# The end of a convolution, attention and expert kernel: the outputs of the experts sorted on TensorE, a new order of the two layers, and more weight buffers

## The chip, the cores and the metric

The kernel runs on one core of a Trainium2 chip. The metric is the device time of one execution in microseconds; the time of a kernel is the median of several runs. Engines are named as in the profile: PE (TensorE), PEld (its weight loads), DVE (VectorE), ACT (ScalarE), POOL (GpSimd), SP (SyncE, which here issues every DMA).

## The reference, cut to what matters

Eight images of 128 channels by 36 by 36 pass through a convolution and attention layer, then through an additive attention over 1296 tokens, and last through a layer of 64 experts, each of which picks 8 tokens of an image. Only the last part is touched in substance:

```
def _L1_ffn_ref(x, gate_w, gate_b, weight1, weight2):
    logits = jnp.einsum('bsd,ed->bse', x, gate_w) + gate_b
    probs = jax.nn.softmax(logits, axis=1)
    vals, idx = jax.lax.top_k(probs.transpose(0, 2, 1), K)      # K = 8 tokens of 1296
    ...
    pooled = jnp.einsum('bked,bke->bed', gathered, topv)        # one row per image and expert
    h = jnp.concatenate([pooled.transpose(1, 0, 2), ones], axis=-1)
    h = jax.nn.gelu(jnp.einsum('ebd,edh->ebh', h, weight1), approximate=False)
    h = jnp.concatenate([h, ones], axis=-1)
    out = jnp.einsum('ebh,eho->ebo', h, weight2)
    ...
    outputs = outputs.at[jnp.arange(Bn)[:, None], flat_idx].add(weighted)   # back to the tokens, by topv
    return outputs
```

`weight1` is 64 experts of 129 x 512 floats and `weight2` is 64 of 513 x 128; the last row of each is a bias. Without the biases they are 32 MiB, and every byte is read once. The result is added to the residual and written as 8 images of 128 x 1296 floats (5.3 MB).

## The kernel before

The order of each engine's instructions is written out by hand: generators are advanced in turn, and nothing is rescheduled afterwards. All DMAs stand in one queue, SP's, in program order. A DMA that must wait for something holds up every DMA behind it. Eight semaphores serve the DMAs in rotation, so each DMA also waits until the one eight places before it has landed.

The long part is the additive attention of layer 1. It is cut into units (image, third of the queries, tile of keys), each unit into 12 slots. In a slot PE makes a denominator `d` and a numerator `n` (L963), ACT takes the logarithm and exponential (`lq`, L986 and L989), and DVE multiplies (L1006 to L1017). The products of four slots are summed on DVE in `accd`, those of the other eight by POOL in `accp` (L1024, L1026). At the end of a unit `sums` folds the two halves of `accp` together and adds `accd`, both on POOL (L1033, L1035), and ACT makes the weights `e` (L1046). The key factors `kf` are loaded two units ahead by `prefetch` (L946). Images overlap: while image b is in this loop, image b+1 goes through its convolutions in the background, which read the padded windows `xwin`.

After the last unit, pools of the loop (`score`) are closed and the pool `wts`, 9 buffers of 1 MiB, takes their place. Nine weight loads are issued (L1202 for `weight1`, L1204 for `weight2`), then the biases, the last piece of the layer's input, 24 loads of gates `gd` (L1224) and the residuals `res` (L1229, L1241). Between these stands the store of image 7's gates (L879). Meanwhile the gating of image 7 ends in `pooled` (L901).

The experts are then worked off in 16 groups of four. For a group there are three steps:

- `inner`: bias by a matmul with a selector `which`, then the first layer, then Gelu on ACT (L1255, L1258, L1261);
- `turned`: four transposes of the hidden values and a copy by DVE (L1268, L1270);
- `outer`: the second layer, 32 matmuls (L1280); four groups share a PSUM bank, and DVE copies it out once in four groups (L1284).

One pass of the loop over g does `outer(g - 2)`, `turned(g - 1)`, `inner(g)` and issues up to two weight loads. Loads stand in the queue as w1[g], w2[g-2], w1[g+1], and so on.

The outputs come out with the image along partitions (32 rows for each of four experts, 8 of them used). They are needed with the expert along partitions, for two images at a time. The kernel writes them to DRAM in one order (`eod`, L1299, four DMAs) and reads them back in another (`eo`, L1305, four DMAs), and DVE adds the second bias (L1306). Last, for each pair of images and each third of the tokens, PE multiplies by the gates (`pf`, L1314), DVE adds to the residual (L1317, 24 times), and an image is stored when its three thirds are done (L1319).

Of the kernel before, what the change touches and what calls it, by code (L numbers as in the profile page):

```python
# [10 lines left out]
F32 = mybir.dt.float32  # L11
# [9 lines left out]
CH = 432  # L21
# [51 lines left out]
def kernel(  # L73
# [53 lines left out]
    ident = const.tile([128, 128], F32, tag="ident", name="ident")  # L127
    make_identity(nc, ident)

    eod = dram.tile([NB, E, O], F32, tag="eod", name="eod")  # L130

    with ExitStack() as loop, ExitStack() as score:

        def pool(name, bufs, stack=loop, side="left", space=bass.MemoryType.SB):
# [4 lines left out]

        big = pool("big", 8, ctx)  # L140
        etp = pool("etp", NKT + 1, ctx)
        chunks = pool("chunks", 8)
        one = pool("one", 1)
        two = pool("two", 2)
        kfp = pool("kfp", 3, score, "right")
        kstp = pool("kstp", 3, score, "right")
# [755 lines left out]
            yield matmuls()  # L902

        res = []

        def residuals(n):

# [83 lines left out]
        def numerators(p):  # L991
            ns = [ps_n.tile([128, 512], F32, tag="n", name="n") for _ in range(banks(*slots[p]))]
            products(*slots[p], 1, ns)
            return [ps[:, :CH] for ps in ns]

        def terms(p, ns):

            u, k = slots[p]
            g, o = group_of[p]
            lq = lq_of[g]  # L1000
            mult = nc.vector.tensor_mul
            rem = units[u][2] == NKT - 1
            if k in DVE_PAIRS and not rem:
                if k == DVE_PAIRS[0]:
                    live["d"] = acc.tile([128, CH], F32, tag="accd", name="accd")
                    mult(live["d"], ns[0], lq[:, o, :])  # L1006
                    mult(ns[1], ns[1], lq[:, o + 1, :])
                    nc.vector.tensor_add(live["d"], ns[1], live["d"])
                else:
                    for h in range(2):  # L1010
                        mult(ns[h], ns[h], lq[:, o + h, :])  # L1011
                    for h in range(2):
                        nc.vector.tensor_add(live["d"], ns[h], live["d"])  # L1013
            else:
                rp = rpp.tile([128, 2, CH], F32, tag="rp", name="rp")
                for h, n in enumerate(ns):
                    mult(rp[:, h, :], n, lq[:, o + h, :])  # L1017
                if rem:
                    live.setdefault("rem", []).extend(rp[:, h, :] for h in range(len(ns)))
                elif k == 0:  # L1020
                    live["r"] = rp
                elif k == 2:
                    live["p"] = acc.tile([128, 2, CH], F32, tag="accp", name="accp")
                    nc.gpsimd.tensor_add(live["p"], live["r"], rp)  # L1024
                else:
                    nc.gpsimd.tensor_add(live["p"], live["p"], rp)  # L1026
            if p in ends:
                lq_of.pop(g)

        def sums(u):  # L1030

            s = live.pop("p")
            nc.gpsimd.tensor_add(s[:, 0, :], s[:, 0, :], s[:, 1, :])  # L1033
            d = live.pop("d")
            nc.gpsimd.tensor_add(d, s[:, 0, :], d)  # L1035
            return d

        es = {}
# [132 lines left out]
        while pending:  # L1171
# [10 lines left out]
        biases = ctx.enter_context(tc.tile_pool(name="biases", bufs=1, side="right"))  # L1182
# [6 lines left out]
        w1s, w2s = {}, {}  # L1189
# [28 lines left out]
        gates = [[etp.tile([128, CH], F32, tag="e", name="gates") for _ in range(NCH)]  # L1218
# [13 lines left out]


    last = ctx.enter_context(tc.tile_pool(name="last", bufs=1))

    def aux(name):
        return ps_last.tile([128, 512], F32, tag="aux", name=name)

    for b in range(len(res), NB):
        res.append(big_tile("res")[:, :N])  # L1240
        nc.sync.dma_start(res[b], t2d[b])  # L1241
    load_gates(NB - 1)

    out_s = last.tile([128, NGR, O], F32, tag="out_s", name="out_s")
    hidden, hidden_t, sums_of = {}, {}, {}

    def inner(g):
        ph = aux("phid")
# [14 lines left out]

    def turned(g):
        x = hidden.pop(g)
        pt = aux("phT")
        for c in range(NHC):
            nc.tensor.transpose(pt[:, c * 128 : (c + 1) * 128], x[:, c::NHC], ident)  # L1268
        xt = hidp.tile([128, NHC, 128], F32, tag="hidT", name="hidT")
        nc.vector.tensor_copy(xt.rearrange("p c b -> p (c b)"), pt)  # L1270
        hidden_t[g] = xt

    def outer(g):
        xt = hidden_t.pop(g)
        if g % 4 == 0:
            sums_of[0] = aux("pout")
        po = sums_of[0][:, (g % 4) * O : (g % 4 + 1) * O]
        for c in range(NHC):
            for q in range(EG):
                mm(po[32 * q : 32 * q + 32, :], xt[:, c, 32 * q : 32 * q + 32],  # L1280
                   w2s[g][:, q, c * O : (c + 1) * O],
                   start=(c == 0), stop=(c == NHC - 1))
        if g % 4 == 3:
            nc.vector.tensor_copy(  # L1284
                out_s[:, g - 3 : g + 1, :], sums_of[0].rearrange("p (g o) -> p g o", o=O)
            )

    for g in range(NGR + 2):
        if 0 <= g - 2:
            outer(g - 2)  # L1290
        if 0 <= g - 1 < NGR:
            turned(g - 1)
        if g < NGR:
            inner(g)
        for _ in range(min(1 + (g >= 2), len(to_load))):
            load_next()
    eods = eod.rearrange("b (g q) o -> q b g o", q=EG)
    for q in range(EG):
        nc.sync.dma_start(eods[q], out_s[32 * q : 32 * q + NB])  # L1299


    eos = []
    for h in range(NB // 2):
        eos.append(last.tile([128, O], F32, tag=f"eo{h}", name="eo"))
# [77 lines left out]
```

## Time and profile before

| | us |
|---|---|
| median of 3 runs | 6135.24 (6124.2 to 6139.08) |
| the profiled execution, its own time | 6138.18 |
| its span in the profile | 6136.4 |
| end of the last unit's sums on POOL (L1035) | at 5989.43 |
| first weight load issued | at 5984.71 |
| `pooled` of image 7 copied (L901) | at 6017.86 |
| first `pf` matmul | at 6115.78 |
| first output store issued | at 6120.67 |

Times "at" are counted from the start of the span. Up to about 5985 us the kernel is in the main loop, where PE is the busiest engine (92% over the whole span); from there on it is in the part described last. In the profile's tables by stage each row has a stretch of time, its length, the busy time of PE, PEld, DVE, ACT and POOL with the number of instructions, the granted PE clock (1.00 is full speed), the busy share of the 16 DMA engines, and GB/s. In the chain of waits each row has a start, a duration and what the end of the run was waiting for at that time.

### The profile page before, as it was taken

To read this page: it belongs to the slowest core of one execution; us is meant where nothing else is said; L and a number is where in the kernel's file an instruction comes from. 1 tells how busy PE (TensorE), PEld (TensorE's weight loads), DVE (VectorE), ACT (ScalarE), POOL (GpSimd) and SP (SyncE) were. 2 spreads that over 40 slices of the span, in tenths; PEclk is the share of its full clock that TensorE was granted. 3 is DMA by queue.
4 is the path that set the end of the run, shared out by engine and by line. 5 is a ranking of instruction groups with operands and counts; after the bars stand their busy time and mean duration, and the time that the engine had idled before them with its cause. 6 is when DMAs were issued, how large, how long until landed. Compare 5 with 4: busy or idle time off the path is not lost.

```text
span 6136.4 us, 94187 instructions
## 1 busy us (share of the span) xinstructions
PE 5669.6 (92%) x33480; PEld 2924.0 (48%) x33480; DVE 4787.2 (78%) x9521; ACT 5331.3 (87%) x5851; POOL 4595.9 (75%) x2819
## 2 busy tenths in 40 slices
PE   7999999999999999999999999999999999988886
PEld 5554455544554445544445444454455544534433
DVE  4787878878788788877788777887878878788882
ACT  1999898998989989889998999899998998999990
POOL 4777777787778867778687777877777777777870
PEclk9999999999999999999999999999999999999997
DMA  1200021001110011100111001110011001110008
GB/s 44 73 34 22 25 75 39 20 25 33 67 38 20 26 47 52 37 24 26 59 37 42 22 20 65 40 37 22 25 67 47 21 25 33 57 49 26 28 20 297
DMA packets 151528, 270.95 MB, mean 44 GB/s; under 512 B 45648, under 2 KB 76752, under 8 KB 151056
## 3 DMA queue, kind: packets, MB, share of 16 engines
q1 hardware_dynamic: 151056, 264.92, 13.0%
q8 instruction: 264, 4.33, 0.3%
q14 instruction: 208, 1.70, 0.1%
HBM read 200.41 MB, written 64.19 MB: 43 GB/s over the span
## 4 chain that ended last, share of the span: by engine, by line
PE 54%; DVE 16%; ACT 15%; issue 11%; POOL 2%; DMA 1%; SPq 0%; DVEq 0%; ACTq 0%; POOLq 0%
PE d L963 18%; PE n L963 12%; ACT lq L986 11%; PE pa L286 7%; DVE rp L1017 7%; DVE n L1011 5%; PE pc L286 5%; PE s L286 3%; DVE accd L1013 2%; PE pq L286 2%; PE pk L286 1%; PE d L968 1%; PE n L968 1%; ACT e L1046 1%; DMA w<-in_weight_dram 1%
## 5 line engine op out<-in xcount | busy, mean ns | idle before, releaser
L1026 POOL TENSOR_TENSOR accp<-accp,rp 128x864 f32<-128x864 f32 x1440 | 2912.8, 2023 | 989.4 <-DVE rp L1017 946.2
L963 PE MATMUL d<-qf,kf 32*128 32x432 f32 (+1 forms) x11520 | 2791.6, 563 | 264.8 <-ACT lq L986 259.6
L963 PE MATMUL n<-qf,kf 32*128 32x432 f32 (+1 forms) x11520 | 3001.7, 556 | 28.4 <-DVE rp L1017 10.0
L986 ACT ACTIVATE lq<-d 128x864 f32<-128x864 f32 x2928 | 2481.1, 877 | 471.2 <-PE n L963 288.8
L1017 DVE TENSOR_TENSOR rp<-n,lq 128x432 f32<-128x432 f32 x3912 | 2182.0, 601 | 760.7 <-PE n L963 606.0
L989 ACT ACTIVATE lq<-lq 128x864 f32<-128x864 f32 (+1 forms) x1944 | 2495.9, 1284 | 61.6
L963 PEld LDWEIGHTS d<-qf,kf 32*128 32x128 f32 (+1 forms) x11520 | 1026.4, 185 | 1445.5 <-ACT lq L986 1106.0
L963 PEld LDWEIGHTS n<-qf,kf 32*128 32x128 f32 (+1 forms) x11520 | 1263.3, 186 | 700.1 <-issue 293.8
L1013 DVE TENSOR_TENSOR accd<-n,accd 128x432 f32<-128x432 f32 x1440 | 867.8, 603 | 24.7
L1011 DVE TENSOR_TENSOR n<-n,lq 128x432 f32<-128x432 f32 x1440 | 810.8, 607 | 58.3 <-PE n L963 36.8
L1024 POOL TENSOR_TENSOR accp<-rp 128x864 f32<-128x864 f32 x240 | 485.1, 2021 | 290.3 <-DVE rp L1017 287.7
L286 PE MATMUL pa<-xh,e 128*108 128x129 f32 x1920 | 254.8, 281 | 35.2 <-DVE accd L1013 28.0
L286 PEld LDWEIGHTS pa<-xh,e 128*108 128x108 f32 x1920 | 221.0, 174 | 129.9 <-DVE accd L1013 103.0
L1035 POOL TENSOR_TENSOR accd<-accp,accd 128x432 f32<-128x432 f32 x240 | 266.1, 1109 | 18.8
L1033 POOL TENSOR_TENSOR accp<-accp 128x432 f32<-128x432 f32 x240 | 264.7, 1103 | 11.9
L713 POOL TENSOR_SCALAR qf<-qf,cs_s 128x432 f32<-128x432 f32 x192 | 260.0, 1364 | 9.3 <-ACT qf L712 9.3
L464 POOL TENSOR_TENSOR tot<-tot,e 116x432 f32<-116x432 f32 x192 | 212.2, 1105 | 9.0 <-ACT e L473 4.6
L286 PE MATMUL s<-q,k 128*116 128x432 f32 x480 | 207.0, 547 | 8.1 <-DVE accd L1013 5.6
L473 ACT ACTIVATE e<-s 116x432 f32<-116x432 f32 x240 | 116.1, 520 | 99.3 <-PE s L286 98.1
L286 PE MATMUL pa<-e,vw 116*128 116x432 f32 x480 | 196.8, 532 | 0.5
L286 PEld LDWEIGHTS pk<-xT,a_k 128*128 128x128 f32 x1408 | 164.9, 193 | 54.2 <-DVE accd L1013 43.5
L1006 DVE TENSOR_TENSOR accd<-n,lq 128x432 f32<-128x432 f32 x240 | 144.1, 600 | 50.1 <-PE n L963 29.7
(213 smaller groups left out, 3796.2 us busy)
## 6 DMA issues: line engine op xcount, KB each, us to landing
kf<-kd SPq DMA_DIRECT2D x239, 512.0 KB
kd<-ks SPq DMA_DIRECT2D x158, 256.0 KB
w<-in_weight_dram SPq DMA_DIRECT2D x32, 1024.0 KB
wk_t<-wk_t_d SPq DMA_DIRECT2D x7, 768.0 KB
wv_t<-wv_t_d SPq DMA_DIRECT2D x7, 768.0 KB
wq_t<-wq_t_d SPq DMA_DIRECT2D x7, 768.0 KB
x<-in_x_dram SPq DMA_DIRECT2D x8, 648.0 KB
t<-tokd SPq DMA_DIRECT2D x96, 54.0 KB
```

What stands on the lines that cost most here:

```text
L286: mm(out, lhsT, rhs, **kw)
L713: nc.gpsimd.tensor_scalar(qf[:, 1, :], qf[:, 0, :], cs_s[:, q : q + 1], None, ALU.mult)
L963: mm(outs[h][:, :CH], kf[rows[h], q, :], qf_of[b, c, q][rows[h], part, :], start=True, stop=True)
L986: nc.scalar.activation(lq[:, o : o + n, :], d[:, :n, :CH], AF.Ln)
L989: nc.scalar.activation(some, some, AF.Exp, scale=-1.0)
L1011: mult(ns[h], ns[h], lq[:, o + h, :])
L1013: nc.vector.tensor_add(live["d"], ns[h], live["d"])
L1017: mult(rp[:, h, :], n, lq[:, o + h, :])
L1024: nc.gpsimd.tensor_add(live["p"], live["r"], rp)
L1026: nc.gpsimd.tensor_add(live["p"], live["p"], rp)
L1033: nc.gpsimd.tensor_add(s[:, 0, :], s[:, 0, :], s[:, 1, :])
L1035: nc.gpsimd.tensor_add(d, s[:, 0, :], d)
```

## The change

Five edits, all in the last part or for its sake:

1. The first group's `weight1`, both biases and so one of the 32 weight loads move forward to the start of image 7's units. They go into `xwin`, which no later convolution needs; the pool `one` is kept open for that.
2. `wts` has 10 buffers, and 10 loads are issued at once (the first of them is now w1[1]).
3. In the very last unit the last addition into `accp` and the two additions of `sums` are done by DVE, not POOL.
4. In the loop over groups `inner(g)` stands ahead of `outer(g - 2)`. Each group's output is copied out by itself, transposed by PE, and copied by DVE to its place in `by_image`. After the loop four more transposes give the expert along partitions, and DVE adds the bias straight from PSUM. `eod` and its eight DMAs are gone. A second PSUM pool of four banks, `ps_more`, is added.
5. In the last stage 8 of the 24 additions to the residual are done by POOL, from a copy that ACT makes (`held`).

```diff
@@ the pools @@
         etp = pool("etp", NKT + 1, ctx)
+        one = pool("one", 1, ctx)
         chunks = pool("chunks", 8)
-        one = pool("one", 1)
...
+        w1s, w2s, ffn_bias = {}, {}, []
+        def first_weights():
+            t = one.tile(list(xwin.shape), F32, tag="xwin", name="w0").rearrange(
+                "p j n -> p (j n)"
+            )
+            w1s[0] = t[:, : EG * HID].rearrange("p (e h) -> p e h", e=EG)
+            nc.sync.dma_start(w1s[0], weight1[:EG, :128, :].rearrange("e d h -> d e h"))
+            b1_s = t[:E, EG * HID : (EG + 1) * HID]
+            nc.sync.dma_start(b1_s, weight1[:, 128, :])
+            b2_s = t[:, (EG + 1) * HID : (EG + 1) * HID + O]
+            for h in range(2):
+                nc.sync.dma_start(b2_s[E * h : E * (h + 1)], weight2[:, HID, :])
+            ffn_bias.extend((b1_s, b2_s))
...
+        def ending(u):
+            return nc.vector if u == len(units) - 1 else nc.gpsimd
...
-                    nc.gpsimd.tensor_add(live["p"], live["p"], rp)
+                    ending(u if k == NP - 1 else 0).tensor_add(live["p"], live["p"], rp)
...
-            nc.gpsimd.tensor_add(s[:, 0, :], s[:, 0, :], s[:, 1, :])
+            ending(u).tensor_add(s[:, 0, :], s[:, 0, :], s[:, 1, :])
             d = live.pop("d")
-            nc.gpsimd.tensor_add(d, s[:, 0, :], d)
+            ending(u).tensor_add(d, s[:, 0, :], d)
...
                     if b == NB - 1:
                         gates.append(residuals(4))
+                        first_weights()
...
-            tc.tile_pool(name="wts", bufs=9, side="right", reuse_waits="tile")
+            tc.tile_pool(name="wts", bufs=10, side="right", reuse_waits="tile")
...
-        for g in range(NGR + 2):
+        for g in range(1, NGR + 2):
...
-        for _ in range(9):
+        for _ in range(10):
             load_next()
-        b1_s = biases.tile([E, HID], F32, tag="b1", name="b1_s")
-        nc.sync.dma_start(b1_s, weight1[:, 128, :])
-        b2_s = biases.tile([128, O], F32, tag="b2", name="b2_s")
-        for h in range(2):
-            nc.sync.dma_start(b2_s[E * h : E * (h + 1)], weight2[:, HID, :])
+        b1_s, b2_s = ffn_bias
...
     def outer(g):
         xt = hidden_t.pop(g)
-        if g % 4 == 0:
-            sums_of[0] = aux("pout")
-        po = sums_of[0][:, (g % 4) * O : (g % 4 + 1) * O]
+        po = aux("pout")[:, :O]
...
-        if g % 4 == 3:
-            nc.vector.tensor_copy(
-                out_s[:, g - 3 : g + 1, :], sums_of[0].rearrange("p (g o) -> p g o", o=O)
-            )
+        of_group = ends_p.tile([128, O], F32, tag="outs", name="outs")
+        nc.vector.tensor_copy(of_group, po)
+        outs.append((g, of_group))
+
+    def sort_outs():
+        g, of_group = outs.popleft()
+        pt = aux("poT", ps_more)[:, :128]
+        nc.tensor.transpose(pt, of_group, ident)
+        nc.vector.tensor_copy(
+            by_image[:, :, g * EG : (g + 1) * EG].rearrange("o b q -> o q b"),
+            pt.rearrange("o (q x) -> o q x", q=EG)[:, :, :NB],
+        )
 
     for g in range(NGR + 2):
+        if g < NGR:
+            inner(g)
         if 0 <= g - 2:
             outer(g - 2)
         if 0 <= g - 1 < NGR:
             turned(g - 1)
-        if g < NGR:
-            inner(g)
+        if len(outs) > 1 or g == NGR + 1:
+            sort_outs()
         for _ in range(min(1 + (g >= 2), len(to_load))):
             load_next()
-    eods = eod.rearrange("b (g q) o -> q b g o", q=EG)
-    for q in range(EG):
-        nc.sync.dma_start(eods[q], out_s[32 * q : 32 * q + NB])
+    while outs:
+        sort_outs()
 
     eos = []
     for h in range(NB // 2):
+        pt = aux("peo", ps_more)[:, :O]
+        nc.tensor.transpose(
+            pt, by_image[:, 2 * h : 2 * h + 2, :].rearrange("o b e -> o (b e)"), ident
+        )
         eos.append(last.tile([128, O], F32, tag=f"eo{h}", name="eo"))
-        nc.sync.dma_start(eos[h], eod[2 * h : 2 * h + 2].rearrange("b e o -> (b e) o"))
-        nc.vector.tensor_add(eos[h], eos[h], b2_s)
+        nc.vector.tensor_add(eos[h], pt, b2_s)
...
-            pfs = [aux("pf")[:, :CH] for _ in range(2)]
+            pfs = [aux("pf", of)[:, :CH] for of in (ps_last, ps_more)]
...
                 r = res[2 * h + i][:, cols]
-                nc.vector.tensor_add(r, pfs[i], r)
+                if i == 1 and c < NCH - 1:
+                    held = ends_p.tile([128, CH], F32, tag="held", name="held")
+                    nc.scalar.activation(held, pfs[i], AF.Copy)
+                    nc.gpsimd.tensor_add(r, held, r)
+                else:
+                    nc.vector.tensor_add(r, pfs[i], r)
```

More of the change, by code (lines that the diff above doesn't have):

```diff
@@ L128 @@
     make_identity(nc, ident)
-    eod = dram.tile([NB, E, O], F32, tag="eod", name="eod")
     with ExitStack() as loop, ExitStack() as score:
@@ L1178 @@
         wts = ctx.enter_context(
-            tc.tile_pool(name="wts", bufs=9, side="right", reuse_waits="tile")
+            tc.tile_pool(name="wts", bufs=10, side="right", reuse_waits="tile")
         )
         hidp = ctx.enter_context(tc.tile_pool(name="hidp", bufs=2, side="right"))
-        biases = ctx.enter_context(tc.tile_pool(name="biases", bufs=1, side="right"))
         ps_last = ctx.enter_context(
@@ L1185 @@
         )
-        w1s, w2s = {}, {}
         to_load = deque()
-        for g in range(NGR + 2):
+        for g in range(1, NGR + 2):
             if g < NGR:
@@ L1234, with aux @@
     last = ctx.enter_context(tc.tile_pool(name="last", bufs=1))
-    def aux(name):
-        return ps_last.tile([128, 512], F32, tag="aux", name=name)
+    ends_p = ctx.enter_context(tc.tile_pool(name="ends", bufs=2))
+    ps_more = ctx.enter_context(
+        tc.tile_pool(name="ps_more", bufs=4, space=bass.MemoryType.PSUM)
+    )
+    def aux(name, of=ps_last):
+        return of.tile([128, 512], F32, tag="aux", name=name)
     for b in range(len(res), NB):
@@ L1242 @@
     load_gates(NB - 1)
-    out_s = last.tile([128, NGR, O], F32, tag="out_s", name="out_s")
-    hidden, hidden_t, sums_of = {}, {}, {}
+    by_image = last.tile([O, NB, E], F32, tag="by_image", name="by_image")
+    hidden, hidden_t, outs = {}, {}, deque()
     def inner(g):
@@ L1265, in turned @@
         x = hidden.pop(g)
-        pt = aux("phT")
+        pt = aux("phT", ps_more)
         for c in range(NHC):
@@ L1292 @@
             turned(g - 1)
-        if g < NGR:
-            inner(g)
+        if len(outs) > 1 or g == NGR + 1:
+            sort_outs()
         for _ in range(min(1 + (g >= 2), len(to_load))):
             load_next()
-    eods = eod.rearrange("b (g q) o -> q b g o", q=EG)
-    for q in range(EG):
-        nc.sync.dma_start(eods[q], out_s[32 * q : 32 * q + NB])
+    while outs:
+        sort_outs()
     eos = []
     for h in range(NB // 2):
+        pt = aux("peo", ps_more)[:, :O]
+        nc.tensor.transpose(
+            pt, by_image[:, 2 * h : 2 * h + 2, :].rearrange("o b e -> o (b e)"), ident
+        )
         eos.append(last.tile([128, O], F32, tag=f"eo{h}", name="eo"))
-        nc.sync.dma_start(eos[h], eod[2 * h : 2 * h + 2].rearrange("b e o -> (b e) o"))
-        nc.vector.tensor_add(eos[h], eos[h], b2_s)
+        nc.vector.tensor_add(eos[h], pt, b2_s)
     for h in range(NB // 2):
```

## The prediction

> **What bounds the kernel now.** I read the table by stage first, over the stretch after the main loop, since every edit lies there (the main loop's instructions keep their order on every engine but for four loads on SP).
>
> ```profile
> 6017.00:6024.00 7.00, 6.28 (x19) 2.56 (x19) 0.70 (x2) 0.60 (x1) 0.29 (x1) 0.50 0.60 164
> 6044.00:6100.00 56.00, 42.57 (x489) 21.55 (x482) 9.17 (x14) 5.97 (x10) 2.58 (x9) 0.94 1.04 384
> 6106.00:6116.00 10.00, 0.21 (x2) 0.24 (x4) 0.58 (x2) 0.00 (x0) 0.00 (x0) 0.63 0.29 47
> 6121.00:6131.00 10.00, 8.40 (x33) 4.41 (x30) 9.42 (x19) 0.00 (x0) 0.00 (x0) 1.00 0.96 378
> ```
>
> From 6044 to 6100 the DMA engines are full at 384 GB/s: the weights set the pace, PE has 13 us to spare. Before that there is a hole at 164 GB/s, from 6106 to 6116 every engine stands nearly still, and from 6121 the output stores fill the DMA engines again. The chain of waits says what the end hangs on in each piece.
>
> ```profile
> 5985.09 2.00 POOL accp L1026
> 5987.16 1.10 POOL accp L1033
> 5988.34 1.09 POOL accd L1035
> ...
> 6083.31 14.52 DMA w<-in_weight_dram
> 6097.83 0.14 issue
> 6097.96 1.08 PE pout L1280 x32
> 6099.04 0.68 PE phT L1268 x4
> 6099.72 1.05 PE phid L1255 x2
> 6100.77 0.99 PE phid L1258 x8
> 6101.77 0.87 PE pout L1280 x32
> ...
> 6104.11 1.12 PE pout L1280 x32
> 6105.26 0.70 DVE out_s L1284
> ...
> 6108.33 4.98 DMA eod<-out_s
> ```
>
> A load takes 14.5 us from issue to landing, so some five are under way and the number of buffers does not limit the steady part. PE starts `outer` on a fresh load at 6081.73, 6087.15, 6092.55 and 6097.96: 5.41 us for two loads, 2.7 each. Two loads follow the one of 6097.83, so the last lands at about 6103.2. Last, the waits of SP's own queue, for what holds the loads up:
>
> ```profile
> SPq L1202 <- POOL accp L1026: 6.8, 1, 6.8
> SPq L1224 <- DMA w<-in_weight_dram: 6.2, 3, 2.8
> SPq L1241 <- DMA gd<-gt: 4.5, 1, 4.5
> ```
>
> The first weight load waits for POOL to have read an `rp` buffer (issue at 5984.71). Then nine loads fill the DMA engines; three gates trickle out behind landing weights; the other 18, then `res`, the store of gates and its landing (4.5 us) keep SP until 6033.86, when the tenth load is issued.
>
> [...]so all of SP's queue stands behind a waiting load. The trace agrees (the 4.5 us at L1241). [...]the four 64 KB stores of `eod` need 4.98 us from the last issue. [...] The trace shows 0.63 from 6106 to 6116 and 1.00 again from 6121.
>
> **Part by part.**
>
> *Last sums on DVE.* Before: 2.00 + 1.10 + 1.09 us on POOL to 5989.43. After: DVE ends the last `rp` at 5984.94 and adds 864, 432 and 432 elements. DVE's 64x1296 SBUF addition (L878) takes 1499 ns, 1.16 ns an element, so 1.0 + 0.6 + 0.6 = 2.2 us, end at 5987.2. The weights `e`, and `pooled` behind them, come 2.2 us earlier. I cost that at nothing for the end: the store of image 7's gates is issued at 6025.03 though its data are ready at 6010.9 (SP is not there yet), and PE's group work is far enough ahead of the loads at 6034. That cover is SP's gate loads; without them it would be worth 2.2 us.
>
> *Tenth buffer.* The tenth buffer makes the pool reach further into the memory of the closed pools. In the changed kernel as built, the first load waits for the last of these DVE additions, because it now overlaps `accd`. So it goes out at 5987.2, not 5984.71: a new wait of **+2.4 us**, and every load and gate is behind it.
>
> *Loads.* Before the gates there are ten loads instead of nine (+2.7) and no biases (192 KB at 384 GB/s, -0.5): the last one before the stall lands +4.6 later. By then six gates have gone out instead of three, as each waits only for an older load; 15 instead of 18 follow, at 0.64 us each (SP's rows of the timeline: 18 issues from 6012.3 to 6024.3, one of them 0.7 longer): -2.0. SP reaches the store of gates, its 4.5 us wait and the next weight load **+2.6 us** later, at 6036.5. But 21 loads are left instead of 23: -5.4. The last load lands at 6100.4, **-2.8 us**. The early load costs 1.2 MB, 3.2 us of DMA time, at the start of image 7; `kf` is loaded two units ahead, a unit takes over 20 us and DMA is 10 to 20% busy there: nothing.
>
> *Order of the loop.* `outer(13)` to `outer(15)` were held by PE, not by the load: `inner(15)` stood between them, and the last `outer` ended at 6105.2, 2.0 us after its load. Now `inner(g)` uses the load that lands first, and `outer(15)` starts on its landing: end 0.14 + 1.08 = 1.2 after it. The added transposes and copies (16 of each, 0.3 us) lie in PE's and DVE's waits for loads; PE has 13 us of idle in 56, they need 5.
>
> *Sorting.* After that `outer`, with 0.06 for a hand-over between engines: DVE copy 0.29 (like L772, 108x129), transpose 0.34 (L1268), DVE copy 0.27 (L901), first of four transposes 0.34, bias 0.29 (L1306), the first pair of `pf` 0.99 (four 64x432 matmuls of L963 in the timeline), two more pairs at 0.9, one DVE addition 0.6. Sum 1.2 + 0.35 + 0.4 + 0.33 + 0.4 + 0.35 + 0.99 + 1.8 + 0.6 = 6.4 us from the landing to the first store. Before: 6120.67 - 6103.2 = 17.5. **-11.1 us**, of which the DRAM trip is some 9.
>
> *Shared additions.* DVE needed 24 x 0.52 us; POOL takes 8 of them at 1.1 us (L1033) after an ACT copy. I count nothing for it beyond the first store: from the first store's issue to the end are 15.7 us, and 5.3 MB at 378 GB/s are 14.0 of them. The stores are the bound, and remain it. POOL ends its eighth addition at 4.0 + 0.65 + 8.9 = 13.6 us after the landing, while the last store's turn comes at about 19; the second store, which waits for POOL's second, is ready 0.6 us after the first, inside the first's 1.7.
>
> **Sum.** -2.8 - 11.1 = -13.9 us. Against the profiled execution's own 6138.18: 6124.3. That one lies 2.9 over the median 6135.24, so the median becomes 6121.3. That is 0.23%; 0.3%, about what a measurement of this kernel can tell from no change, would be 18.4 us.
>
> **Rivals.**
> - *The loads gain in full.* If the first load does not wait for the sums in effect, or the gates hide behind the tenth load, the stream gains up to 5.9 us, and with a quicker hand-over in the sorting the sum is -17 to -20: 6115 to 6118. For it: SP's 0.64 us gates leave the DMA engines at 164 GB/s. Against it: SP stands in order.
> - *Half clock at the end.* The sorting leaves PE little to do for 2 us; if the clock falls, the pairs of `pf` take 1.8 us, above the 1.1 that the stores need, for 3 to 10 us (both lengths occur): +3 to +6, 6124 to 6128. For it: the clock fell to half at 6043 and 6071 in the loop.
> - *Slower.* The early load stands in SP's queue ahead of `kf`. If its buffer were still being read, all of image 7's `kf` loads would wait; slower by 0.3% needs a stall of 32 us, so a hold of over 70. Against it: the last read of `xwin` is at 5019, over 200 us earlier.
> - *No change at all.* All of it hidden: excluded by the 10 idle us before 6116 on the chain.
>
> **Chances.** The sum as worked out 0.55 (its own range 6116 to 6127), full gain 0.25, half clock 0.15, slower 0.03, the rest unexplained. The bound lies at 6116.8, in the full gain and the lower edge of the sum, to which the runs' own spread of 15 us adds: faster 0.29, within 0.68, slower 0.03. The range reaches from 6109 to 6131.
>
> **What would show it.** Right: first load issued near 5987, next load after the gates near 6036.5, last `pout` ending near 6101.6, first `pf` near 6103.4, first store near 6106.8, span near 6122.5, no `eod`. Wrong: a first load at 5984.7, an end that hangs on POOL `res` or on PE `pf` at half clock, or main loop times that moved.

## The result, and the profile after

The changed kernel takes 6122.38 us in the median of 22 runs, against 6132.9 us of the kernel before, also 22 runs: a ratio of 0.9983, interval 0.9977 to 0.9989, that is 10.5 us less (7 to 14). The profiled execution took 6131.19 us with a span of 6129.5.

Executions of one and the same kernel differ by some 20 us. Nearly all of it arises in the main loop, which the change leaves alone: in the profiled executions shown here its last `rp` addition on DVE ended between 5972.8 and 5990.4 us, later where the record of the granted clock has more time at half clock (116 us of it in the one case, 172 in the other). In the profile before it ended at 5984.94, in the profile after at 5989.94. All places below are therefore counted from the end of that addition, and **the rest** is the time from there to the end of the span: 151.5 us before, 139.5 after.

| us after the last `rp` | before | predicted | after |
|---|---|---|---|
| first weight load issued | -0.2 | 2.3 | 2.5 |
| last load of the first row landed (9th, after: 10th) | 27.3 | 31.9 | 35.0 |
| next weight load, behind the gates | 48.9 | 51.6 | 54.3 |
| last weight load landed | 118.2 | 115.5 | 117.7 |
| first `pf` matmul | 130.8 | 118.5 | 120.7 |
| first output store issued | 135.7 | 121.9 | 123.8 |
| end (the rest) | 151.5 | 137.6 | 139.5 |

The table by stage of the changed kernel, with the columns as before (stretch, length, busy PE, PEld, DVE, ACT, POOL, PE clock, DMA share, GB/s):

```profile
6025.00:6035.00 10.00, 10.00 (x70) 3.56 (x73) 1.68 (x3) 2.83 (x4) 0.86 (x3) 0.77 0.58 155
...
6050.00:6106.00 56.00, 42.22 (x497) 22.01 (x497) 11.29 (x31) 5.38 (x9) 2.02 (x7) 0.91 1.03 380
6107.00:6113.00 6.00, 4.71 (x52) 2.91 (x54) 2.77 (x9) 1.06 (x2) 0.70 (x1) 1.00 0.01 3
6114.00:6124.00 10.00, 5.58 (x32) 2.70 (x28) 6.66 (x13) 3.10 (x6) 6.93 (x7) 0.89 0.95 375
```

The hole at the gates is still there, 155 GB/s for 10 us. The ten idle microseconds before the last stage are gone: from 6107 to 6113 the DMA engines rest, but PE is busy 4.71 of 6 us, at full clock. The chain of waits shows what it does, from the landing of the last load to the first `pf`:

```profile
6092.79 14.86 DMA w<-in_weight_dram
6107.65 0.14 issue
6107.78 1.11 PE pout L1294 x32
6108.90 0.02 issue
6108.92 0.30 DVE outs L1298
6109.23 0.04 issue
6109.27 0.34 PE poT L1304
6109.61 0.02 issue
6109.64 0.22 DVE by_image L1305
6109.86 0.04 issue
6109.90 0.34 PE peo L1327
6110.25 0.02 issue
6110.27 0.30 DVE eo L1331
6110.57 0.04 issue
6110.61 1.05 PE pf L1339 x4
```

Each link takes a few tenths of a microsecond where a trip through DRAM stood. The first store is issued at 6113.73, 6.1 us after the landing (before: 17.5). From the first store to the end are 15.8 us, as before (15.8): one store lands every 1.67 us. SP's own waits name what became worse:

```profile
SPq L1217 <- DVE accd L1051: 66.0, 1, 66.0
...
SPq L1235 <- DMA w<-in_weight_dram: 8.5, 3, 5.2
...
SPq L1257 <- DMA gd<-gt: 4.8, 1, 4.8
```

SP has nothing to do ahead of the first load, so the length of the first wait says nothing; what ends it does: the last sum (L1051), 2.5 us after the last `rp`. The wait of the gates for landing weights has grown from 6.2 to 8.5 us, and one wait of it is now 5.2 us.

### The profile page after: what moved, and what is told of

It is laid out like the page before. It is cut to its first block, busy times and chain, and to the rows that moved or that the text cites. A ratio compares the mean times of both kernels' runs of the same rounds, so it can differ in the third digit from the quotient of the medians.

```text
span 6129.5 us, 94280 instructions
## 1 busy us (share of the span) xinstructions
PE 5669.4 (92%) x33500; PEld 2928.9 (48%) x33500; DVE 4786.5 (78%) x9544; ACT 5338.2 (87%) x5859; POOL 4603.0 (75%) x2824
## 4 chain that ended last, share of the span: by engine, by line
PE 54%; DVE 16%; ACT 15%; issue 11%; POOL 2%; DMA 1%; SPq 0%; DVEq 0%; POOLq 0%; ACTq 0%
PE d L976 18%; PE n L976 12%; ACT lq L999 11%; PE pa L284 7%; DVE rp L1033 7%; PE pc L284 5%; DVE n L1027 5%; PE s L284 3%; DVE accd L1029 2%; PE pq L284 2%; PE pk L284 1%; PE d L981 1%; PE n L981 1%; ACT e L1062 1%; DMA w<-in_weight_dram 1%
## 5 line engine op out<-in xcount | busy, mean ns | idle before, releaser
L1042 POOL TENSOR_TENSOR accp<-accp,rp 128x864 f32<-128x864 f32 x1439 | 2912.2, 2024 | 995.3 <-DVE rp L1033 951.4
L976 PE MATMUL n<-qf,kf 32*128 32x432 f32 (+1 forms) x11520 | 2997.9, 556 | 31.0 <-DVE rp L1033 12.4
L1051 POOL TENSOR_TENSOR accd<-accp,accd 128x432 f32<-128x432 f32 x239 | 265.4, 1110 | 18.7
L471 ACT ACTIVATE e<-s 116x432 f32<-116x432 f32 x240 | 116.3, 521 | 99.1 <-PE s L284 97.9
```

What stands on the lines that cost most here:

```text
L976: mm(outs[h][:, :CH], kf[rows[h], q, :], qf_of[b, c, q][rows[h], part, :], start=True, stop=True)
L1042: ending(u if k == NP - 1 else 0).tensor_add(live["p"], live["p"], rp)
L1051: ending(u).tensor_add(d, s[:, 0, :], d)
```

## The experiments

All numbers but the ratios are microseconds after the last `rp` of the profiled execution; the rest is a length from there. The ratio is to the kernel before; each of the others without a ratio ran once, for its profile.

| kernel | first load | next load behind the gates | last load landed | first store | rest | ratio |
|---|---|---|---|---|---|---|
| before | -0.2 | 48.9 | 118.2 | 135.7 | 151.5 | |
| changed | 2.5 | 54.3 | 117.7 | 123.8 | 139.5 | 0.9983 |
| sums_on_pool | 4.5 | 55.9 | 119.3 | 126.4 | 142.1 | |
| nine_buffers | -0.2 | 45.3 | 111.7 | 117.8 | 133.6 | |
| nine_timed | -0.2 | 46.0 | 111.7 | 117.8 | 133.5 | 0.9967 |
| old_loop_order | 2.5 | 53.3 | 116.1 | 123.4 | 139.1 | |
| all_sums_on_dve | 2.5 | 53.3 | 117.9 | 124.6 | 140.4 | |
| sort_only | -0.2 | 47.7 | 116.3 | 124.2 | 140.0 | 0.9984 |
| loads_spread | 2.5 | 40.6 | 118.7 | 125.9 | 141.7 | |
| spread_and_early | -0.2 | 38.4 | 117.5 | 123.6 | 139.3 | 0.9979 |
| wide_gates | -0.2 | 39.0 | 104.7 | 110.8 | 126.4 | 0.9966 |
| wide_and_tenth | -0.2 | 41.5 | 105.2 | 112.3 | 127.9 | 0.9963 |
| wide_spread | -0.2 | 38.4 | 109.7 | 115.8 | 131.4 | |
| store_early | -0.2 | 38.6 | 105.2 | 112.3 | 127.9 | 0.9960 |

Two executions of the kernel with nine buffers have the same rest to 0.1 us; elsewhere the next load behind the gates moved by about 1 us between executions with the same loads (54.3 and 53.3). Differences of the rest under 1 us are not read. A ratio over five runs has an interval of some 15 us, so that most differences among the later kernels rest on the profiles alone.

### The parts of the change, one by one

**Sorting alone** (the diff's edit 4 without the new order of the loop, on the kernel before):

```diff
+        of_group = ends_p.tile([128, O], F32, tag="outs", name="outs")
+        nc.vector.tensor_copy(of_group, po)
+        outs.append((g, of_group))
...
-        nc.sync.dma_start(eos[h], eod[2 * h : 2 * h + 2].rearrange("b e o -> (b e) o"))
-        nc.vector.tensor_add(eos[h], eos[h], b2_s)
+        nc.tensor.transpose(
+            pt, by_image[:, 2 * h : 2 * h + 2, :].rearrange("o b e -> o (b e)"), ident
+        )
+        nc.vector.tensor_add(eos[h], pt, b2_s)
```

> The kernel before with one part of the change, the sorting of the outputs on TensorE; the order of the loop, 9 buffers, the weights of the first group and the biases, the sums and all additions to the residual stay as before. My theory: nearly the whole gain is this part. The last load lands as before, 118.2 us after the last rp addition; from there 1.2 us more than the 21.8 of the changed kernel for the order of the loop and 0.7 more for the additions all on DVE. Expected: first output store 8.9 us earlier than before (126.8 us after the last rp), rest 141.9 us against 151.5, ratio 0.9984. Rival: part of the gain came from the loads; then the rest is 145 us or more and the ratio 0.999 or more.

Measured: rest 140.0, ratio 0.9984 (0.9977 to 0.9990), the same as the whole change. The first store follows the last landing after 7.9 us, against 17.5 before: 9.6 of the 11.5 us. The other 1.9 are an earlier last landing, for which this edit gives no reason. So this one part is worth as much as the whole change, and the other four edits together come out at nothing that the times can tell.

**The additions shared out**, undone:

```diff
-                if i == 1 and c < NCH - 1:
+                if False:
```

> The changed kernel with all 24 additions to the residual on DVE, none on ACT and POOL. My theory: the output stores are the bound (one lands every 1.67 us), DVE needs 24 x 0.55 = 13 us for the additions. Expected: first store 0.4 us later (five additions ahead of it, not three), last store landing 0.4 us later, rest 139.9 us. Rival: DVE's additions from PSUM take 0.6 us or more and set the pace (14.4 us and more); then the stores are more than 1.67 us apart and the rest is 141 to 142 us.

Measured: the first store 6.7 us after the last landing instead of 6.1, the end 22.5 after it instead of 21.8: 0.7 us worse, near the first figure. The view of the tile `res`, first of the changed kernel, then of this one (durations are smallest, median, largest in ns, then the first and last start):

```profile
L1347 DVE TENSOR_TENSOR res<-pf,res x16: 595/597/606, 6111.6 to 6120.1; 128x432 f32<-128x432 f32 x16
L1345 POOL TENSOR_TENSOR res<-held,res x8: 1098/1101/1105, 6112.3 to 6119.9; 128x432 f32<-128x432 f32 x8
L1349 SPq DMA_DIRECT2D out_dram<-res x8: 332/646/1166, 6113.7 to 6121.3; - x8
```

```profile
L1347 DVE TENSOR_TENSOR res<-pf,res x24: 586/590/606, 6102.2 to 6114.0; 128x432 f32<-128x432 f32 x24
L1349 SPq DMA_DIRECT2D out_dram<-res x8: 332/340/589, 6104.9 to 6114.7; - x8
```

24 additions of 0.59 us, which overlap a little (one starts every 0.52 us), end 12.4 us after the first starts, and the stores, 1.67 us each, are still not done then. DVE is not the bound, as the prediction had it; what the sharing brings is the first store 0.6 us earlier.

**The order of the loop**, undone:

```diff
     for g in range(NGR + 2):
-        if g < NGR:
-            inner(g)
         if 0 <= g - 2:
             outer(g - 2)
         if 0 <= g - 1 < NGR:
             turned(g - 1)
+        if g < NGR:
+            inner(g)
```

> The changed kernel with outer(g - 2), turned(g - 1), inner(g) in the old order; the sorting after inner. My theory: PE is held at the last groups by inner(15) between the second layers, as in the kernel before, where outer(15) ended 2.0 us after its load had landed; in the changed kernel it is 1.2 us. Expected: last pout ends 2.0 us after the last landing, rest 140.3 us; loads not moved. Rival: the order sets which buffers come free first, so that the stream of loads itself slows down in the old order; then the last landing is later than 117.7 by a load (2.7 us) or more.

Measured: the last `pout` ends 2.4 us after the last landing instead of 1.2, as the first theory says. But the last landing itself is at 116.1, 1.6 to 1.8 us *earlier* than in the two executions with the new order and the same loads (117.7, 117.9), so the rest is no worse. The rival had the loads move the other way. The next load behind the gates is at 53.3 here and in all_sums_on_dve, so the difference arises in the loop. There SP's waits in the new order are for the first layer (`phid`, L1274: 13.7 us in all_sums_on_dve), in the old one mostly for other work of PE. With one execution of each, and the clock dropping at different times, it stays open whether the order costs what it gains.

**The last sums on POOL again:**

```diff
-            return nc.vector if u == len(units) - 1 else nc.gpsimd
+            return nc.gpsimd
```

> The changed kernel with the last three sums of the last unit on POOL again; all else as changed. I measure from the end of the last rp addition on DVE to the end of the span (the rest): 151.5 us before, 139.5 after. My theory: with ten buffers the first weight load waits for the last of these sums, so the edit is worth what it shortens this wait. Expected: first load 4.5 us after the last rp (2.5 in the changed kernel), every later load and the end 2.0 us later, rest 141.5; pooled of image 7 is copied 33.2 us after the last rp instead of 31.1. Rival, as the prediction had it: SP's gate loads hide it and the rest stays at 139.5, with the first load at 4.5 or not.

SP's waits from 9 us before the last `rp` to 21 after it:

```profile
SPq L1217 <- DVE rp L1033: 63.6, 1, 63.6
SPq L1217 <- POOL accd L1051: 4.5, 1, 4.5
```

Measured: first load at 4.5, `pooled` at 33.2, next load 1.6 us later and last landing 1.6 us later than in the changed kernel. The rest is 2.6 us longer; the missing 1.0 is the clock, which was at half for 3.4 us from 114.2 and made the last `outer` end 2.2 us after its load instead of 1.2. So with ten buffers this edit is worth some 1.6 us, not nothing: it shortens a wait that the tenth buffer has made. With nine buffers it was not undone.

**Nine buffers instead of ten**, twice:

```diff
-            tc.tile_pool(name="wts", bufs=10, side="right", reuse_waits="tile")
+            tc.tile_pool(name="wts", bufs=9, side="right", reuse_waits="tile")
...
-        for _ in range(10):
+        for _ in range(9):
             load_next()
```

> The changed kernel with 9 weight buffers and 9 loads at once instead of 10. My theory: the tenth buffer pushes the first load behind the sums and the gates behind one more load, and the steady part never lacks a buffer. Expected: first load 0.2 us before the last rp (2.5 after it in the changed kernel), next weight load after the gates at 49 us after the last rp (54.3), but 22 loads left instead of 21, so that the last load lands 2.6 us earlier (115.1, not 117.7) and the rest is 137.0 us, not 139.5. Rival: the tenth buffer is worth its load; then the rest is 2.7 us longer, 142.2.

Measured: rest 133.6, 6.0 us shorter than with ten, where I had worked out 2.6. SP's waits:

```profile
SPq L1217 <- POOL accp L1042: 6.8, 1, 6.8
...
SPq L1235 <- DMA w<-in_weight_dram: 5.4, 3, 2.2
SPq L1257 <- DMA gd<-gt: 3.9, 1, 3.9
```

The first load waits as before the change (L1042 is the earlier L1026), and the gates wait 5.4 us for weights, none longer than 2.2, instead of 8.5 with one of 5.2. The seventh gate goes out at 26.5, on the landing of the ninth load (each DMA waits for the one eight places before it); with ten buffers at 35.0, on that of the tenth. Of these 8.5 us, 2.7 are the first wait and 2.7 the load; 3.0 I had not counted. The trace's semaphore updates show them: 15 of 16 DMA engines end the tenth load at 31.5 to 32.0, one at 35.0, and that one stays behind the others for all six gates that follow. The DMA view of the changed kernel has, between 6019 and 6025 us, one packet of another queue (packets, MB, share of 16 engines):

```profile
q1 hardware_dynamic: 1031, 1.71, 99.8%
q8 instruction: 1, 0.02, 1.1%
```

It is 16 KB, starts at 29.7 and takes 1.05 us. Every profiled execution has such a packet, starting between 29.2 and 31.8. In the changed kernel the ninth load has landed by then (29.3), the tenth has not. In the kernel with nine buffers the gates in flight at that time end on one engine some 1.2 us later than on the others. The other profiles with ten first loads agree. In the five where the tenth load is in flight when the packet comes (changed, sums_on_pool, old_loop_order, all_sums_on_dve, loads_spread), it ends on one engine 3.0, 2.4, 2.1, 2.0 and 0.9 us after the other 15. In the three where it has landed by 29.4, ahead of the packet (spread_and_early, wide_and_tenth, wide_spread), all 16 end within 0.6 us. That the packet puts the engine back I infer from this; the trace does not tell which engine the packet ran on, nor why the delay is up to three times the packet's own time.

> The changed kernel with 9 weight buffers, as in nine_buffers, timed. There the rest was 133.6 us, 6.0 shorter than with ten buffers, 3.4 more than I had worked out. My theory: the tenth load was still under way when PE's instruction fetch (16 KB at 29.7 us after the last rp) delayed one DMA engine by 2 to 3 us, and SP waited for just this load; the ninth has landed before. Expected: rest 133 to 134.5 again, gates 7 and later going out from 26.5 us, ratio to the kernel before 0.997. Rival: chance of one execution; then the rest is 136 to 140 and the ratio that of the changed kernel, 0.9983.

Measured: rest 133.5, the seventh gate at 26.6, last landing 111.7; ratio 0.9967 (0.9955 to 0.9979). The cost is no chance of one execution: as the change has it, with the wait that it brings, the tenth buffer costs 6 us, about what the weight load moved ahead of the loop and the other edits bring. The times agree, though this interval just touches that of the changed kernel (0.9977 to 0.9989).

### Where the gates' time goes

**The loads spread.** After the first row of loads, everything that does not have to come at once is issued in turns with weight loads:

```diff
-        for b in range(NB - 1):
-            load_gates(b)
         res.append(big_tile("res")[:, :N])
         nc.sync.dma_start(res[4], t2d[4])
+        for b in range(4):
+            drain(load_gates(b))
         drain(gate_tokens(NB - 1))
...
         for _ in range(min(1 + (g >= 2), len(to_load))):
             load_next()
+            next(others, None)
```

> The changed kernel with another order of SP's queue after the ten first loads: res of image 4 and the gates of images 0 to 3, then the store of image 7's gates; the other 15 loads (res 5, gates of 4 to 6, res 6 and 7, gates of 7) one by one behind the weight loads of the loop over groups. My theory: the time from the tenth landing to the next weight load (54.3 us after the last rp) is SP's own, 21 gates at 0.64 us and 5 us of waiting for the store of gates; with a weight load always under way the DMA engines stay full, the last of them lands 103.6 us after the last rp (117.7 in the changed kernel) and the rest is 125.5 us. Rival: PE's first groups, which free the buffers, are the limit: the first buffer is free 38.6 us after the last rp and then two come free every 3.7 us; then loads land later and the gain is 5 us or less, rest over 134.

and, with the tenth buffer in a pool of its own behind a ring of nine,

```diff
+        tenth = ctx.enter_context(tc.tile_pool(name="tenth", bufs=1, side="right"))
...
-        for _ in range(10):
-            load_next()
+        for i in range(10):
+            load_next(tenth if i == 9 else wts)
```

> As loads_spread, and the first load freed of its wait: a ring of 9 weight buffers and a tenth one by itself, which lies deepest in memory and is used once, for the tenth load. My theory: first load 0.2 us before the last rp (2.5 after it in the changed kernel) and, as the DMA engines never stop, every later load and the end 2.7 us earlier too: rest 122.8 us, and with the mean of all runs a ratio of 0.9953. Rival: with the loads 2.7 us earlier PE becomes the limit at the start, and the rest is as without it (125.5).

Measured: 141.7 and 139.3, no gain at all, though SP issues the next weight load at 40.6 and 38.4 instead of 54.3. My theory that the stall was SP's own fell, and so did the rival in part: PE does hold the next loads up (SP waits 20.7 us for it from 26 to 116 in spread_and_early), but the stream is slow for 40 us after that too. A stretch of 36 us from the loop, in the table by stage of spread_and_early:

```profile
6031.59:6067.59 36.00, 32.70 (x368) 16.38 (x356) 8.80 (x24) 4.61 (x8) 2.30 (x8) 0.88 1.05 315
```

The DMA engines are fully busy and move 315 GB/s; with weights alone they move 386 (changed kernel, 70 to 105 us after the last `rp`). The packets tell why: in this stretch the 2048-byte packets of the weights take 109 ns on average, with weights alone 88; around most loads of gates their average over half a microsecond rises to 120 to 165 ns.

**Wide loads of gates.** The gates are loaded to 64 partitions at a time, the weights to 128. That the 64 partitions slow the packets was my guess; the runs so far had not shown it. In the next four kernels two images lie side by side in DRAM, so that one load of gates goes to 128:

```diff
+    gd2 = [dram.tile([2 * E, N], F32, tag=f"gd{h}", name=f"gd{h}") for h in range(NB // 2)]
+    gd = [gd2[b // 2][E * (b % 2) : E * (b % 2) + E] for b in range(NB)]
...
-        def load_gates(b):
-            half = slice(E * (b % 2), E * (b % 2) + E)
+        def load_gates(h):
             for c in range(NCH):
-                nc.sync.dma_start(gates[b // 2][c][half], gd[b][:, c * CH : (c + 1) * CH])
+                nc.sync.dma_start(gates[h][c], gd2[h][:, c * CH : (c + 1) * CH])
```

First spread as before, to see the packets:

> As spread_and_early, with gates loaded for two images at a time: 128 partitions instead of 64. In spread_and_early the DMA engines were full, but at 315 GB/s instead of 386: whenever a load of gates was under way, the 2048-byte packets of the weights took 130 to 165 ns instead of 88. My theory: it is the 64 partitions of the gates[...]; loads of 128 partitions do not disturb. Expected: weight packets at 88 to 95 ns throughout, last landing at 104 us after the last rp (117.5 there), rest 126 us. Rival: it is the mixing of two sources or packet sizes; then the packets are as slow as before for as many bytes, and the rest is 136 us or more.

The same 36 us of the loop:

```profile
6030.50:6066.50 36.00, 31.09 (x392) 16.33 (x384) 8.80 (x24) 5.21 (x9) 2.30 (x8) 0.98 1.04 379
```

379 GB/s, and 90 ns for the packets of weights; after the first 3 us of the stretch no average over half a microsecond is above 97 (within them one reaches 208). So it is not the mixing of two sources or packet sizes. What changed with the 64 partitions is the number of gate loads, half as many of twice the size, and the place of the gates in DRAM; the packets kept their 1728 bytes. The rest, 131.4, lies between the two expectations, since the start of the loop is still slow (272 GB/s from 6020.5 to 6030.5, PE at 0.65 of its clock): there PE has not freed buffers, and the gates that could fill the time have been put off.

> The changed kernel with 9 weight buffers and the gates of two images side by side in DRAM, so that one load of 128 partitions takes the place of two of 64: 12 gate loads instead of 24, same bytes, same place in SP's queue. My theory: SP's stall between the first loads and the next one (45.3 us after the last rp with nine buffers) is the number of SP's instructions. 9 gates instead of 21 ahead of the store of gates at 0.64 us each: it is reached 7.7 us earlier; the next weight load is issued at 38 to 39, where PE frees the first buffer, and the last one lands at 104.5 to 105 (111.7 with nine buffers). Expected rest 126.5 us, ratio to the kernel before 0.996. Rival, from the two runs with the loads spread: while gates are under way all packets are slow, whatever SP does, so that the transfers only crowd together; then the next weight load is issued at 43 or later and the rest is 131 us or more.

This kernel, like store_early below, has nine buffers. Measured: next load at 39.0, last landing 104.7, rest 126.4, each as expected, and 7.1 us less than with nine buffers and loads of 64 partitions. SP's rows of the timeline show the nine loads of gates, the wait for the store within `res`, and the next weight load:

```profile
6008.07 10.34 SPq L1235 DMA_DIRECT2D gates<-gd  x9
6018.63 0.32 SPq L1240 DMA_DIRECT2D res<-t2d  x1
6019.29 0.52 SPq L878 DMA_DIRECT2D gd<-gt  x1
6019.90 7.62 SPq L1257 DMA_DIRECT2D res<-t2d  x3
6027.58 1.69 SPq L1235 DMA_DIRECT2D gates<-gd  x3
6029.36 0.43 SPq L1218 DMA_DIRECT2D w<-in_weight_dram  x1
```

The 1728-byte packets of the gates take 75 ns here (27 to 40 us after the last `rp`); in the changed kernel they take 100 (36 to 44), with nine buffers 121 (27 to 36). Fewer issues and faster packets come together in this kernel; how much each is worth was not separated. The 7.1 us are the profiles' alone: the ratio, 0.9966 (0.9953 to 0.9978), cannot be told from nine_timed's 0.9967.

> As wide_gates, with a tenth buffer by itself, deepest in memory and used once, for the tenth load. The first load then does not wait for the sums (0.2 us before the last rp). My theory: the tenth load fits into the time in which PE has not freed a buffer yet (38.6 us after the last rp), and one load less is left: last landing 2.7 us earlier than in wide_gates, rest 124 us. Rival: the tenth load pushes the gates and the store back by its own 2.7 us; then the rest is that of wide_gates or longer (126 to 129).

Measured: next load at 41.5, 2.5 us later, and last landing 105.2: the rival. The rest is 127.9; of the 1.5 us more, 1.0 is the clock, at half from 100.0 to 103.4, after which the last `pout` ended 2.2 us after its load. Here a tenth load gains nothing: the DMA engines have other work (329 to 404 GB/s from 24 to 38, in steps of 2 us) until PE frees buffers.

> As wide_gates, with the store of image 7's gates directly behind the first three gate loads instead of behind nine of them and res of image 4. There SP waited 6.8 us for the store to land (issued 28.9 us after the last rp, next issue 36.3), and the DMA engines moved 334 GB/s instead of 387 meanwhile. My theory: the store's data are ready 23.9 us after the last rp, so it goes out at 24.0 to 24.5 and has landed by 32; the last loads of res and gates go out by 36, the next weight load at 38.4 to 39 as PE frees its buffer, but with less in front of it: it lands at 44.4 instead of 46.5, rest 124.3 us (126.4 in wide_gates), ratio to the kernel before 0.996. Rival: PE sets the pace from there (its first groups run at half clock), so that the earlier loads only wait; then the rest stays at 126 to 127.

```diff
-        for h in range(NB // 2 - 1):
+        load_gates(0)
+        drain(gate_tokens(NB - 1))
+        for h in range(1, NB // 2 - 1):
             load_gates(h)
         res.append(big_tile("res")[:, :N])
         nc.sync.dma_start(res[4], t2d[4])
-        drain(gate_tokens(NB - 1))
```

Measured: rest 127.9, the rival's mechanism again, and 1.0 of it is the same half clock from 100.0 to 103.4. Three rows of its table by stage, the first 27 to 40 us after the last `rp`, the next 42 to 46, the last 50 to 100:

```profile
5999.82:6012.82 13.00, 13.00 (x43) 6.21 (x44) 0.61 (x2) 2.48 (x3) 0.57 (x2) 0.50 1.04 393
6014.82:6018.82 4.00, 4.00 (x45) 2.33 (x38) 0.33 (x2) 0.60 (x1) 0.00 (x0) 0.58 0.66 182
6022.82:6072.82 50.00, 43.32 (x527) 21.76 (x526) 12.48 (x35) 7.17 (x12) 2.87 (x10) 1.00 1.05 386
```

The hole at the store is filled (393 GB/s, 333 in wide_gates), but another has come from 42 to 46: SP now waits 4.5 us for the first layer, and PE is busy all the time but at half clock until 45.4. In wide_gates the clock was back at 39.6. What the earlier store is worth where the clock comes back as early, one execution of each does not tell. Both kernels beat the one before: 0.9966 (0.9953 to 0.9978) and 0.9960 (0.9946 to 0.9974), some 21 to 25 us less. The second interval lies clear of the changed kernel's, the first just touches it; they cannot be told from each other, nor from wide_and_tenth at 0.9963 (0.9949 to 0.9976) or nine_timed.

## Why the prediction was right, and where its steps failed

The median was forecast at 6121.3 and is 6122.4, the change at -13.9 and is -10.5 with an interval that reaches to -14; the rest of the profiled execution fell by 12.0. That the median came within 1.1 us is in part luck: the forecast started from 6135.2, the median of three runs, and that of 22 is 2.3 lower. In the rest the sum is 1.9 off: it has the last load of the first row land 3.1 too early, and what follows made up 1.2.

- **Sorting, -11.1: right.** From the last landing to the end the profile has 33.27 us before and 21.83 after, -11.4. The first `pf` came 3.0 us after the landing as worked out (1.2 + 0.35 + 0.4 + 0.33 + 0.4 + 0.35), the first store 6.1, not 6.4. Not all of the gain is the trip through DRAM: from the first `pf` to the first store it took 4.9 us before, with the clock at half until 133.9, and takes 3.1 now, at full clock (3.7 in sort_only, which does not share the additions). sort_only shows that the part stands by itself. The stores remained the bound.
- **Tenth buffer, +2.4: right** (+2.7), and it is its doing: with nine the load goes out at -0.2.
- **Loads, "the last one before the stall lands +4.6 later": the step that failed.** It landed 7.7 later. The tenth load was under way when the 16 KB packet of the `instruction` queue came (29.7), and SP waited for one engine that was late, 3.0 us after the others; that the packet made it late is inferred. From there on the sum was nearly followed: 15 gates instead of 18, next load +5.3 instead of +2.6. The 21 loads that remained took 63.5 us where 23 had taken 69.3, -5.8 (-5.4 worked out). The last landing is at -0.5, not -2.8.
- **The tenth buffer as a whole: mis-sized.** In the sum it costs 2.4 and 2.7 ahead of the gates and saves 2.7 at the other end. Against nine buffers it costs 6.0: the 3.0 of the late engine come on top, and the edit would have been better left out.
- **Last sums on DVE, nothing: wrong by 1.6.** The cover that I named, SP's gate loads, is behind the first load, and that waits for these sums. The next step of my own text had that wait, and did not go back to this one.
- **Order of the loop: half right.** The time from the last landing to the end of the last `pout` fell from 2.4 (old_loop_order) to 1.2, but the loads did not land where they did in the old order.
- **Early load of the first group: nothing, as far as seen.** The load is issued in the first unit of image 7, and the first two units take 19.6 to 19.7 and 24.4 to 24.5 us in every profile, with it or, in sort_only and the kernel before, without. It was not tried alone.
- **The rivals.** Half clock between the last landing and the first store, as I had put it, is in no profile of a kernel that sorts on PE; the changed kernel's clock fell at 131.9, when PE's last product was done (129.6). Half clock in the loop shortly before the end did cost about 1 us in four of them (sums_on_pool, loads_spread, wide_and_tenth, store_early). The full gain of the loads failed on the wait of the first load, as the argument against it said, and on the stall. The slower rival, a held queue ahead of `kf`, left no mark.

SP's order, on which I leaned, held: a wait moved from one place of its queue came back at the next (4.8 us for the store in the changed kernel, then 4.5 for PE in store_early).

## What to carry to other kernels

Count a stall of the queue from the *slowest* of the DMA engines of the load that it waits for, and ask before adding a buffer what its memory overlaps and whether anything is short of it: here one engine was 3.0 us behind the others, and the tenth buffer cost 6 us. Loads to 64 partitions were not only slow themselves here (packets of 100 to 121 ns against 75), the packets of the weights took 120 to 165 ns instead of 88 around most of them; when DMA engines are busy but GB/s is low, look at the packet times before the issue order. And try the parts of a change one at a time: one of five was worth as much as all together, and the sum was right for partly wrong reasons.

## What the hardware showed that I had not expected

- Around most loads of gates to 64 partitions the packets of the weights took 120 to 165 ns instead of 88 (spread_and_early); with loads of the same data to 128 partitions they took 90 on average over the same stretch (wide_spread). The gates' own packets took 100 to 121 ns with 64 partitions (changed, nine_buffers) and 75 with 128 (wide_gates). With the partitions the number of the loads and the place of the gates in DRAM changed too; which of them does it was not separated.
- Packets of 16 KB in a queue that the profile calls `instruction` appear in the trace of the changed kernel once in some 16 us while PE works through the groups (at 50.5, 66.9, 83.3, 99.2 and 115.5), and take about 1.1 us. The whole execution has 264 of them and 67 000 matmuls and weight loads of PE, some 254 to a packet; that they bring PE's instructions, as I had put it in nine_timed, fits this, but the trace does not name the engine that they are for. One of them coincided with a 3.0 us delay of a load that everything waited for.
- Away from the end of the span, each stretch of half clock in the profiles before and after is a multiple of 3.41 us long (3.4, 6.8, 10.2, 41.0 and 44.4). The clock did not come back soon after PE had become busy: from 24 us after the last `rp` PE was busy for 15.99 of 16 us in wide_gates and for 21.99 of 22 in store_early, and full clock came at 39.6 and at 45.4. The products' own times agree: in the changed kernel, whose clock came back at 39.7, those of 128x512 elements took 1061 ns ahead of it, 592 to 617 after. PE was not always idle ahead of a fall: in the kernel before it was busy for 1.80 of the 3.41 us ahead of the fall at 86.1, and for 0.26 ahead of that at 58.8.
